# Long rows' lists in another order, in a kernel of four graph layers

## The chip, the cores and the metric

The kernel runs on one core of one Trainium2 chip. The core has five engines that run their own instruction streams in order and meet at semaphores: TensorE (PE, with the weight loads as PEld), VectorE (DVE), ScalarE (ACT), GpSimd (POOL) and SyncE (SP). SP issues nearly all of the plain transfers of this kernel, POOL the indirect ones. The metric is the device time of one execution in microseconds (us).

## The reference

There are 16 graphs of 1024 nodes with 64 features. Each graph has a sparse adjacency of 1024 x 1024; node i and node j are joined with a chance that falls with both numbers, so low nodes have long rows. Four layers follow each other, each with `h = relu(layernorm(x))` and a residual sum:

- layer 0: `m` from two dense steps of `h`, `msg = relu(adj @ m)`, then a gated unit (sigmoid and tanh) of `msg` and `h`;
- layer 1: `adj + 1` scaled on both sides by the root of the row sums, times `h @ kernel`;
- layer 2: of each node's neighbours some are removed by rank (where there are more than 10), and of the others' `h` a weighted sum of the quantiles 0.25, 0.5 and 0.75 is taken per feature, with interpolation; then two dense steps;
- layer 3: `(adj + 1) @ h` over its row sum.

Layer 2 is the one that matters here. Cut to its core:

```python
vals = jnp.where(valid[..., None], x[:, None, :, :], big)
sv = jnp.sort(vals, axis=2)
...
for tau, wt in zip(TAUS, QWEIGHTS):
    pos = jnp.clip(tau * (mf - 1.0), 0.0)
    ...
    q = gather(lo) * (1.0 - frac) + gather(hi) * frac
    agg = agg + wt * q
```

## The kernel before, in words

**Stages.** Each graph goes through thirteen stages, which are written as generators: fetch and load (read adj in strips of 128 rows, transpose it on PE, write adjT to DRAM), code, rank and cut (pack the neighbour flags into codes, rank the nodes by degree, remove neighbours), list (turn codes into lists of neighbour numbers), mid and next (layers 0 and 1; next ends with `tab`, the table of `h` rows in DRAM), gath (gather neighbours' rows from `tab`), sort and smalls (sort the gathered rows), sums (weighted sums into `agg`), rear (gather `agg` rows by rank into `zz`, layer 2's dense steps, layer 3). The graphs overlap: up to six have their tables in DRAM at once.

**Ranks and rows.** Nodes are ranked by degree. The first 128 ranks are the long rows, called heavy. Their lists have up to 143 entries and are gathered by 26 indirect transfers a graph into buffers `gh`; `gather_heavy` (L1584) issues them on POOL, PE transposes them and ACT copies them into `hb`, which DVE sorts. There are four `gh` buffers, each filled by two transfers. The other ranks, called light, are gathered by 49 transfers into `s` and two into `px`. At the end of a graph POOL gathers `zz` in eight transfers.

**The list stage, `lists` (L1135).** It reads `keys` (128 ranks x 128 codes for each of eight tiles of ranks). For the heavy tile the first 24 ranks (`HASHED`) are too long for 32 entries and are cut in segments, which `cuts` writes to DRAM as `seg` and reads back, spread over all partitions, as `sg2`. In the order of the program before:

1. `KH`: the 32 largest codes of each heavy row (four rounds of maximum and replacement, `rounds`); `KL`: the same for the light tiles.
2. The second round for ranks 24 to 127: `ch` decodes `KH` into 256 entries, four rounds find the 32 largest, `LH` holds them as numbers. The change calls these the far segments.
3. `sg2` is masked, `sc` holds its entries, and rounds find `LA` (32) and `LB` (16), the near lists of the segments of ranks 0 to 23.
4. ACT counts the entries of `LA`, `LB` and `LH` into `cs`; PE sums the counts over segments into `pl`; DVE makes `wa`, `wb_` from `LA`, `LB`, then `before` and `place` from `pl`; `m0` (in `mm`) is the row's length.
5. PE moves the segments' entries to their places, ACT copies them to `LC`.
6. `KL` is decoded into `cd`; flags; then the lists are written to the DRAM tensor `idx` in the order of `PARTS` (L53): 9 small transfers from `LC` and 7 from `LH`, in one loop on SP, after `LC`.
7. The light lists (`LF`, `L`, `idxL`), then `ih` reads `idx` back, PE transposes it, DVE copies it to `idxH`, which holds the gathers' row numbers. Then the weights `wl` and `w`.

A gather of a graph can start when its `idxH` and its `tab` are there and the light gathers of the graph before have been issued.

**What sets the order.** No order is written out by hand. `Order.run` (L278) keeps, for each stage, the next step: the engine that it is for and the tiles that it waits for. It takes the stage with the smallest value of `start` (when the planner's own clock says that the engine is free and the tiles ready) plus `lead`, and lets it emit instructions up to its next `yield`. So a negative lead puts a stage's steps earlier in the engine's stream. The table `LEAD` (L222) has an entry for a kind of stage: five leads for DVE, ACT, PE, POOL and SP in this order; a slope by graph number; four additions for the first four graphs; two for the last two. "stream0", "stream1" and "stream3" are the loads of adjT rows (`am`, three buffers) for layers 0, 1 and 3; "flag" and "keep" run once. What is emitted first for an engine runs first on it, whatever the chip's times are.

Of the kernel before, what the change touches and what calls it, by code (L numbers as in the profile page):

```python
# [9 lines left out]
F32 = mybir.dt.float32  # L10
F16 = mybir.dt.float16
# [4 lines left out]
AF = mybir.ActivationFunctionType  # L16
ALU = mybir.AluOpType
AX = mybir.AxisListType

P = 128  # L20
# [24 lines left out]
HASHED = 24  # L45
WIDE = 160
# [110 lines left out]
def in_two_buffers(lens, kept, moves, first=None):  # L157
# [62 lines left out]


LEAD = {  # L222
    "rear": ((-0.25, -0.25, 0.25, -11, -65.5), -0, (0, -0, -0, -0), (-0.75, -6.5)),
    "gath": ((-11, 0, 0, -4.5, 0.25), -0, (-1.5, -0, 0, 0), (0, -0.25)),
    "sums": ((0, 0, 4, 21.75, -163.5), 0, (-0.75, 0, -0.75, 0), (0, 21.25)),
    "next": ((0, 0, 0, 14, 1.25), -0, (-0.5, 0, -0, 0), (0, 0)),
    "mid": ((0, -0, 0, 1, 4), 0, (-1, 0, -0, 0), (-0, 0)),
    "code": ((-192, -107.5, -0.25, 10, 0), 0, (5, 0, 1, -2), (3, 0)),
    "rank": ((0, 0, -121.5, 9.5, 7.75), 0, (-3.25, 0, 0, -0), (0, 0)),
    "cut": ((0, -1.25, -95.25, 0, -83.75), 0, (0, 0, 0, 0), (0, -0)),  # L230
    "list": ((-0, -3.5, -1, -10, -33.5), 0, (1, 0, -0, 0), (0, 0)),
    "fetch": ((-68.25, -2.25, -21.25, -29.5, -149.75), 0, (-10.5, -31.25, 0, -1.75), (2, 16)),
    "load": ((-49.75, 0, -163, -2.75, 1.25), 0, (-7.75, -0.5, 0, 0), (1, 1)),
    "sort": ((0, -79.5, -0.5, 21.25, -30.5), -0, (0, 0, 0, 0), (0.25, -0.75)),
    "smalls": ((0, 12.25, 7.5, 1.25, 1.5), 0, (0, 0, 0, 0), (-1.75, 1)),
    "flag": ((4, -17, -4.25, -1.75, -4.5), 0.1, (0, 8.5, 0, -8), (0, 0.75)),
    "keep": ((23, -0.75, 32.5, 4.25, -26), -1.55, (-9.75, -22.25, 7.25, 3.5), (15, 3.75)),
# [3 lines left out]
}  # L241


# [227 lines left out]
def kernel(  # L471
# [127 lines left out]
    def lists_for_all():  # L599
        order = Order(B)  # L600
        V, A, T = Engine(nc.vector, "V", order), Engine(nc.scalar, "A", order), Engine(nc.tensor, "T", order)
        G_, S_ = Engine(nc.gpsimd, "P", order), Engine(nc.sync, "S", order)
# [5 lines left out]
        ap_, wp, qp = pool("ap", 1), pool("wp", 1), pool("qp", 1)  # L608
# [59 lines left out]
        for k in range(8):  # L668
            v = NBITS * 2.0**k
# [116 lines left out]
        net16, at16, _ = in_two_buffers((16,), (16,), NET16)  # L786
# [348 lines left out]
        def lists(b, S):  # L1135
            d = D[b % DEPTH]
            info, keys, sg2, raw = S["info"], S["keys"], S["sg2"], I32
            def decoded(dst, codes, n):

                y = dst.rearrange("p (n k) -> p n k", k=8)  # L1140
                k = codes[:, :, None].to_broadcast([P, n, 8])
                p8, c8 = (c[:, None, :].to_broadcast([P, n, 8]) for c in (dpow, dcol))
                V.tensor_tensor(y.bitcast(raw), k.bitcast(raw), p8.bitcast(raw), ALU.bitwise_and)
                yield ("V",)
                V.tensor_sub(y, y, c8)
                yield ("V",)

            fl = ap_.tile([P, 10 + NT], F32, name="fl", bufs=2)

            KH = ap_.tile([P, 32], F32, name="KH", bufs=1)  # L1150
            mk = ap_.tile([P, P], F32, name="mk", bufs=1)
# [3 lines left out]
            for t in range(1, NT):  # L1155
                yield ("V",)
                mk = ap_.tile([P, P], F32, name="mk", bufs=1)
                yield from rounds(ROUNDS[t], KL[:, COFF[t] : COFF[t] + CODES[t]], keys[:, t, :], mk)
            ch = ap_.tile([P, 256], F32, name="ch", tag="cd", bufs=1)
            yield from decoded(ch, KH, 32)  # L1160
            KH = ap_.tile([P, 32], F32, name="KH", bufs=1)
            mh = ap_.tile([P, 256], F32, name="mh", tag="mk", bufs=1)
            yield from rounds(4, KH, ch, mh)
            LH = ap_.tile([P, 32], F16, name="LH", bufs=2)
            V.tensor_scalar(LH, KH, 0.0, None, ALU.max)
            yield ("V",)

            yield "V", sg2
            V.tensor_tensor(
                sg2.bitcast(raw), sg2.bitcast(raw),  # L1170
# [7 lines left out]
            LA = ap_.tile([P, 32], F16, name="LA", bufs=2)  # L1178
# [4 lines left out]
            yield from rounds(2, LB, sc[:, 1, :], mra)  # L1183

            cs = ap_.tile([P, 3], F32, name="cs", bufs=2)
            for i, v in enumerate((LA, LB, LH)):
                ja = ap_.tile([P, 32], F16, name="ja", bufs=1)
                A.activation(ja[:, 0 : v.shape[1]], v, AF.Sign, accum_out=cs[:, i : i + 1])
            c16 = ap_.tile([P, 2], F16, name="c16", bufs=2)
# [10 lines left out]
            for w, v, k in ((wa, LA, SEG_A), (wb_, LB, SEG_C)):  # L1200
                V.tensor_tensor(
                    w, v[:, 0:k, None].to_broadcast([P, k, 16]),
                    bsel[:, 0, None, 0:16].to_broadcast([P, k, 16]), ALU.mult,
                )
                yield ("V",)
            yield "V", pl
            before = ap_.tile([P, 2], F32, name="before", bufs=2)
            V.tensor_scalar(before, pl[:, 2:4], float(SEG_A + 1), None, ALU.add)
# [28 lines left out]
            V.reduce_max(fl[:, 8:9], fe, AX.X)  # L1237
            yield ("V",)
            V.tensor_copy(fl[:, 9:10], LB[:, SEG_C : SEG_C + 1])
            yield "S", LC  # L1240
            base = 0
            for a0, n, e0, k, _, _ in PARTS:
                o = d["idx"][:, base : base + n * k].rearrange("h (a k) -> a h k", k=k)
                for src, col, lo, hi in ((LC, 0, 0, 16), (LC, WIDE, 16, HASHED), (LH, 0, HASHED, P)):
                    r0, r1 = max(lo, 2 * a0), min(hi, 2 * a0 + 2 * n)
                    if r0 < r1:
                        q = 0 if lo == HASHED else lo
                        S_.dma_start(
                            o[r0 // 2 - a0 : r1 // 2 - a0], src[r0 - q : r1 - q, col + e0 : col + e0 + k]
                        )  # L1250
                base += n * k
            for t in range(1, NT):
                o = OFFS[t] + 1
                ml = ap_.tile([P, P], F32, name="ml", tag="mk", bufs=1)
# [1287 lines left out]
```

## Time and profile before

| what | us |
|---|---|
| median of 5 runs | 2279.26 (2274.99 to 2291.03) |
| profiled execution | 2277.36 |
| its span, first to last instruction | 2275.2 |
| DVE busy | 1906.9 |
| POOL busy | 1523.2 |
| first heavy gather (`gh`) of graph 0 starts | 157.5 |
| last light gather (`s`) of graph 15 ends | 2212.9 |
| list of graph 0: first `KH` maximum to `idxH` | 100.1 to 148.5 |
| list of graph 2: the same | 323.4 to 410.7 |

All instructions that the planner emits carry one line number in the profile, that of a helper (L465), so the profile is read by tiles: `gh<-tab,idxH` is a heavy gather, `idx<-LC` a transfer of segments' lists. A wait is put down to the instruction or transfer that came last. The time of a POOL gather is that of writing its descriptors, not of the data's arrival.

### The profile page before, as it was taken

The page shows a single profiled execution, that of the slowest core. Times are in us where ns is not written, and L with a number is a line of the kernel's source. Part 1 is how long each engine was busy: PE and PEld are TensorE (multiplying, and loading weights), DVE is VectorE, ACT ScalarE, POOL GpSimd, SP SyncE. Part 2 cuts the span into 40 slices and gives each one's busy share as a digit, 9 for nine tenths or more (in the row PEclk, how much of TensorE's full clock was granted, in tenths as well). Part 3 has the DMA queues.
Part 4 walks back from the last instruction along what each step waited for, and adds up shares of the span by engine and source line. Part 5 has one row for each costly group of instructions (what it writes and reads, how often), then busy time and mean ns, then how long its engine had stood idle before and what let it go on. Part 6 is the DMA issues. An engine that isn't in the chain of part 4 may idle for free. (4 is left out here: it accounts for less than half of the span.)

```text
span 2275.2 us, 35564 instructions
## 1 busy us (share of the span) xinstructions
PE 1520.7 (67%) x9522; PEld 789.6 (35%) x9522; DVE 1906.9 (84%) x6317; ACT 1538.4 (68%) x5241; POOL 1523.2 (67%) x1428
## 2 busy tenths in 40 slices
PE   4876757676667767687776867666777575763324
PEld 3433324333343433334333433233343233331202
DVE  3546898898988988978998898899889899989882
ACT  6776786787777676768686677777766677554231
POOL 5017767466776776757676777777777677777771
PEclk6887777787777868677877778787877676785565
DMA  7766657677757766776766776876766666463441
GB/s 206 219 210 194 188 149 218 190 189 234 210 155 228 205 165 203 211 230 182 236 192 191 196 219 174 240 208 174 221 166 203 179 185 162 125 171 79 103 148 25
DMA packets 402724, 419.80 MB, mean 185 GB/s; under 512 B 176236, under 2 KB 313330, under 8 KB 402514
## 3 DMA queue, kind: packets, MB, share of 16 engines
q1 hardware_dynamic: 357426, 372.68, 53.6%
q0 software_dynamic: 45088, 44.75, 10.6%
q8 instruction: 78, 1.28, 0.2%
q14 instruction: 132, 1.08, 0.2%
HBM read 332.94 MB, written 84.34 MB: 183 GB/s over the span
## 5 line engine op out<-in xcount | busy, mean ns | idle before, releaser
L465 POOL DMA_INDIRECT s<-tab,idxL x784 | 867.0, 1106 | 239.0 <-issue 228.3
L465 POOL DMA_INDIRECT gh<-tab,idxH x416 | 449.7, 1081 | 340.3 <-DMA tab<-h 119.2
L465 DVE TENSOR_TENSOR hb<-hb 128x128 f32<-128x128 f32 (+10 forms) x1040 | 522.7, 538 | 17.4 <-ACT hb L465 12.8
L465 PE MATMUL bank<-ident,a 128*128 128x128 f32 x1024 | 197.0, 332 | 105.2 <-DMA a<-in_adj_dram 55.6
L465 POOL DMA_INDIRECT zz<-agg,posi x128 | 140.7, 1100 | 120.1 <-issue 35.1
L465 PE MATMUL bank<-am,tr 128*64 128x512 f32 x512 | 173.9, 793 | 65.8 <-DMA am<-adjT 33.9
L465 PE MATMUL bank<-am,hr 128*64 128x512 f32 x480 | 161.7, 780 | 79.8 <-ACT hr L465 44.1
L465 PE MATMUL bank<-am,m2x 128*64 128x512 f32 x512 | 165.0, 728 | 53.2 <-DMA am<-adjT 46.8
L465 PEld LDWEIGHTS bank<-ident,a 128*128 128x128 f32 x1024 | 142.3, 170 | 158.2 <-issue 55.3
L465 ACT COPY strip<-bank 128x512 f32<-128x512 f32 x256 | 146.7, 592 | 62.0 <-PE bank L465 47.4
L465 DVE TENSOR_TENSOR hb<-hb,hb 128x488 f32<-128x488 f32 (+7 forms) x368 | 173.4, 483 | 4.5
L465 ACT ACTIVATE s<-s,wl 128x64 f32<-128x64 f32 x624 | 166.7, 349 | 8.5 <-DVE s L465 8.5
L465 ACT ACTIVATE junk<-bank,nkey 128x1024 bf16<-128x1024 f32 x128 | 142.2, 1111 | 23.6 <-PE bank L465 21.4
L465 ACT ACTIVATE sgn<-strip,flat 128x1024 bf16<-128x1024 f32 x128 | 147.5, 1152 | 4.2 <-PE bank L465 1.2
L465 PE MATMUL bank<-cx,oh 128*128 128x133 f16 (+1 forms) x1280 | 144.1, 263 | 8.1 <-DVE oh L465 7.2
L465 PE MATMUL bank<-ident,gh 128*128 128x128 f32 x208 | 66.9, 346 | 122.0 <-DMA gh<-tab,idxH 115.1
L465 PEld LDWEIGHTS <-oh 128*128 128x128 f16 x1280 | 97.7, 110 | 46.6 <-issue 16.2
L465 DVE TENSOR_TENSOR o<-s 128x64 f32<-128x64 f32 (+6 forms) x208 | 95.2, 490 | 13.7 <-ACT s L465 7.4
L465 PE MATMUL bank<-wg,cat 128*128 128x256 f32 x256 | 99.0, 523 | 0.0
L465 PEld LDWEIGHTS bank<-ident,gh 128*128 128x128 f32 x208 | 31.2, 160 | 181.9 <-issue 134.1
L465 DVE TENSOR_TENSOR s<-o 128x192 f32<-128x192 f32 (+5 forms) x224 | 93.9, 447 | 0.0
L465 PE MATMUL bank<-am,ones 128*32 128x256 f32 x1024 | 92.1, 435 | 0.0
(443 smaller groups left out, 3737.9 us busy)
## 6 DMA issues: line engine op xcount, KB each, us to landing
am<-adjT SPq DMA_DIRECT2D x376, 512.0 KB
a<-in_adj_dram SPq DMA_DIRECT2D x128, 512.0 KB
adjT<-strip SPq DMA_DIRECT2D x128, 512.0 KB
s<-tab,idxL POOLq DMA_INDIRECT x784
gh<-tab,idxH POOLq DMA_INDIRECT x416
wb<-wd SPq DMA_DIRECT2D x32, 152.0 KB
X<-in_x_dram SPq DMA_DIRECT2D x16, 256.0 KB
x<-X SPq DMA_DIRECT2D x16, 256.0 KB
```

Source lines behind the costliest of these rows:

```text
L465: return f(*args, **kw)
```

## The change

Two things change. In `lists`, the second round of the far segments (step 2 above, from `ch` to `LH`) moves behind `wa` and `wb_`, just ahead of the wait for `pl`; ACT's count of `LH` moves with it. The transfers to `idx` are issued in two loops, all 7 from `LH` as soon as it is there and then the 9 from `LC` when that is there. And all 18 entries of `LEAD` have other numbers, so the order of all engines' streams is planned anew. The operations and their number stay.

```diff
 LEAD = {
-    "rear": ((-0.25, -0.25, 0.25, -11, -65.5), -0, (0, -0, -0, -0), (-0.75, -6.5)),
-    "gath": ((-11, 0, 0, -4.5, 0.25), -0, (-1.5, -0, 0, 0), (0, -0.25)),
-    "sums": ((0, 0, 4, 21.75, -163.5), 0, (-0.75, 0, -0.75, 0), (0, 21.25)),
...
-    "list": ((-0, -3.5, -1, -10, -33.5), 0, (1, 0, -0, 0), (0, 0)),
-    "fetch": ((-68.25, -2.25, -21.25, -29.5, -149.75), 0, (-10.5, -31.25, 0, -1.75), (2, 16)),
...
-    "stream0": ((6, 0, 0, 2.5, -14.75), -0.15, (-9.25, 16.75, 0, 7.5), (-2.25, 2)),
-    "stream1": ((8.75, -6, 11.25, 13.25, -2), 0.1, (3.5, 2.25, 0.75, -13.75), (-4.5, -5.75)),
-    "stream3": ((-2.75, -4.75, -23, 1.75, -52.5), 1.5, (0.5, 0.5, 0, -6.25), (-27, -8.5)),
+    "rear": ((-0.25, -0, 0.25, -12, 0), 0, (0, 0, 0, 0), (-2, -7.25)),
+    "gath": ((-26, -0.25, -0.25, -4.5, -0.75), 0, (-1.5, 0, 0, 0), (0, 0)),
+    "sums": ((0, 0, -9.75, 4.75, -175.5), -0, (-0.5, 0, -0, 0), (0.25, 37)),
...
+    "list": ((0, -3.5, -1, 0, -143.5), 0, (1, 0, 0, 0), (0, 0)),
+    "fetch": ((-65.5, 6, -1.5, -14.25, -207.75), 1.6, (0.5, 2, 8, -1), (2, 6.5)),
...
+    "stream0": ((6.5, -12.25, 11.25, 5.5, -44.5), 0.4, (8, -4.75, 33.75, 0), (-2.75, 0)),
+    "stream1": ((-10.25, -0, 11.5, -0, -2.25), -0.25, (-5.75, 3, 1.25, 2.75), (1.5, -1.5)),
+    "stream3": ((22.5, 5, 3.25, 4.5, -142.25), 2.5, (0, -1.75, -4, -6.5), (6.5, 0)),
 }
...
                 yield from rounds(ROUNDS[t], KL[:, COFF[t] : COFF[t] + CODES[t]], keys[:, t, :], mk)
-            ch = ap_.tile([P, 256], F32, name="ch", tag="cd", bufs=1)
-            yield from decoded(ch, KH, 32)
-            KH = ap_.tile([P, 32], F32, name="KH", bufs=1)
-            mh = ap_.tile([P, 256], F32, name="mh", tag="mk", bufs=1)
-            yield from rounds(4, KH, ch, mh)
-            LH = ap_.tile([P, 32], F16, name="LH", bufs=2)
-            V.tensor_scalar(LH, KH, 0.0, None, ALU.max)
-            yield ("V",)
-
             yield "V", sg2
...
-            for i, v in enumerate((LA, LB, LH)):
+            for i, v in enumerate((LA, LB)):
                 ja = ap_.tile([P, 32], F16, name="ja", bufs=1)
                 A.activation(ja[:, 0 : v.shape[1]], v, AF.Sign, accum_out=cs[:, i : i + 1])
...
+            ch = ap_.tile([P, 256], F32, name="ch", tag="cd", bufs=1)
+            yield from decoded(ch, KH, 32)
+            KH = ap_.tile([P, 32], F32, name="KH", bufs=1)
+            mh = ap_.tile([P, 256], F32, name="mh", tag="mk", bufs=1)
+            yield from rounds(4, KH, ch, mh)
+            LH = ap_.tile([P, 32], F16, name="LH", bufs=2)
+            V.tensor_scalar(LH, KH, 0.0, None, ALU.max)
+            yield ("V",)
+            ja = ap_.tile([P, 32], F16, name="ja", bufs=1)
+            A.activation(ja, LH, AF.Sign, accum_out=cs[:, 2:3])
             yield "V", pl
...
-            yield "S", LC
-            base = 0
-            for a0, n, e0, k, _, _ in PARTS:
-                o = d["idx"][:, base : base + n * k].rearrange("h (a k) -> a h k", k=k)
-                for src, col, lo, hi in ((LC, 0, 0, 16), (LC, WIDE, 16, HASHED), (LH, 0, HASHED, P)):
-                    r0, r1 = max(lo, 2 * a0), min(hi, 2 * a0 + 2 * n)
-                    if r0 < r1:
-                        q = 0 if lo == HASHED else lo
-                        S_.dma_start(
-                            o[r0 // 2 - a0 : r1 // 2 - a0], src[r0 - q : r1 - q, col + e0 : col + e0 + k]
-                        )
-                base += n * k
+            for src, ways in ((LH, ((0, 0, HASHED, P),)), (LC, ((0, 0, 0, 16), (WIDE, 16, 16, HASHED)))):
+                yield "S", src
+                base = 0
+                for a0, n, e0, k, _, _ in PARTS:
+                    o = d["idx"][:, base : base + n * k].rearrange("h (a k) -> a h k", k=k)
+                    for col, q, lo, hi in ways:
+                        r0, r1 = max(lo, 2 * a0), min(hi, 2 * a0 + 2 * n)
+                        if r0 < r1:
+                            S_.dma_start(
+                                o[r0 // 2 - a0 : r1 // 2 - a0], src[r0 - q : r1 - q, col + e0 : col + e0 + k]
+                            )
+                    base += n * k
```

More of the change, by code (lines that the diff above doesn't have):

```diff
@@ L222 @@
 LEAD = {
-    "rear": ((-0.25, -0.25, 0.25, -11, -65.5), -0, (0, -0, -0, -0), (-0.75, -6.5)),
-    "gath": ((-11, 0, 0, -4.5, 0.25), -0, (-1.5, -0, 0, 0), (0, -0.25)),
-    "sums": ((0, 0, 4, 21.75, -163.5), 0, (-0.75, 0, -0.75, 0), (0, 21.25)),
[L226 to L230, printed above, removed]
-    "list": ((-0, -3.5, -1, -10, -33.5), 0, (1, 0, -0, 0), (0, 0)),
-    "fetch": ((-68.25, -2.25, -21.25, -29.5, -149.75), 0, (-10.5, -31.25, 0, -1.75), (2, 16)),
[L233 to L237, printed above, removed]
[3 rows of a table removed]
+    "rear": ((-0.25, -0, 0.25, -12, 0), 0, (0, 0, 0, 0), (-2, -7.25)),
+    "gath": ((-26, -0.25, -0.25, -4.5, -0.75), 0, (-1.5, 0, 0, 0), (0, 0)),
+    "sums": ((0, 0, -9.75, 4.75, -175.5), -0, (-0.5, 0, -0, 0), (0.25, 37)),
+    "next": ((0, 0, 0, 9, 1.25), 0, (-0.5, 0, 0, 0), (-0.25, 0)),
+    "mid": ((0, 0, 0, -19.75, 3.25), 0, (-1, 0, 0, 0), (0, 0)),
+    "code": ((-383.75, -129.5, -0.25, -8.25, -5.75), 0, (4.5, 0, 1, -87.75), (0.5, -13.5)),
+    "rank": ((-0.5, 0, -146.25, 0.75, 6.75), 0, (-4.25, -1.5, 0, -0), (0, 0)),
+    "cut": ((0, -1.25, -79, -7.5, -88.25), 0, (0.25, 0.5, 0, 0), (0, -0)),
+    "list": ((0, -3.5, -1, 0, -143.5), 0, (1, 0, 0, 0), (0, 0)),
+    "fetch": ((-65.5, 6, -1.5, -14.25, -207.75), 1.6, (0.5, 2, 8, -1), (2, 6.5)),
+    "load": ((-12, 0, -167.5, -9, 1.25), 0, (-3.5, -0.5, 0, 0), (0, 1.5)),
+    "sort": ((0, -75.5, -58.75, 7.5, -50.25), 0, (0, 0, -0, 0), (0.75, -1.5)),
+    "smalls": ((0, 17, -1.75, 1.5, 0), 0, (0, 0, 0, 0), (-2, -28.5)),
+    "flag": ((-56.5, -1.75, 23.75, -4, 0), 2, (-1.75, -0.75, 4.75, -2.5), (11.5, -3.25)),
+    "keep": ((19.5, 29.25, 5.25, 26, 2.75), -0.15, (40.5, -3.25, -9, 3.5), (-0.5, -6.25)),
[3 rows of a table added]
 }
```

## The prediction

> **What bounds the kernel now.** I read the busy shares first, then the stretch between the first and the last gather, then POOL's own waits, and last the timelines of the two places where POOL waits for what a list hands over. Part 1 of the page and the windows view (PE, PEld, DVE, ACT, POOL, PE clock, DMA share, GB/s):
>
> ```profile
> PE 1520.7 (67%) x9522; PEld 789.6 (35%) x9522; DVE 1906.9 (84%) x6317; ACT 1538.4 (68%) x5241; POOL 1523.2 (67%) x1428
> 157.00:2213.00 2056.00, 1389.33 (x8620) 714.60 (x8619) 1818.09 (x5836) 1414.47 (x4898) 1485.81 (x1352) 0.76 0.66 188
> ```
>
> Shares alone name DVE. But POOL's 1352 gathers between 157 and 2213 us each have a gap of 0.30 us ahead of them that is put down to issue: 1485.8 + 1352 x 0.30 = 1891 us, 92% of the 2056, against DVE's 1818 (88%). From graph 3 on, the first heavy gather of a graph (tile gh) starts 0.3 to 2.6 us after the last light gather (tile s) of the graph before: 545.5 to 545.8, 671.2 to 671.5, and so on to 2094.7 to 2095.0. So POOL is the chain: 157.5 us until it can begin, 2055 us of gathers in order, and 62 us after the last light gather. Inside the 2056 us it waits 2056 - 1891 = 165 us. POOL's waits (us in total, times, longest):
>
> ```profile
> POOL s L465 <- issue: 228.3, 749, 0.3
> POOL gh L465 <- DMA tab<-h: 119.2, 1, 119.2
> POOL gh L465 <- PE bank L465: 99.3, 58, 10.9
> POOL zz L465 <- DVE hb L465: 28.9, 5, 9.9
> POOL zz L465 <- DMA agg<-s: 20.2, 2, 18.1
> POOL gh L465 <- DVE idxH L465: 9.8, 2, 9.3
> ```
>
> The second line is the start-up. The third is the ring of four gh buffers that PE's transposes empty. The last is the only line that names a list's result: one wait of 9.3 us, at graph 2, for idxH. Graph 2 in the timelines of SP, PE and POOL:
>
> ```profile
> 388.54 1.39 SPq L465 DMA_DIRECT2D idx<-LC  x2
> 390.04 0.65 SPq L465 DMA_DIRECT2D idx<-LH  x1
> ...
> 398.55 0.62 SPq L465 DMA_DIRECT2D idx<-LC  x1
> 399.28 0.39 SPq L465 DMA_DIRECT2D a<-in_adj_dram  x1
> 399.76 0.39 SPq L465 DMA_DIRECT2D adjT<-strip  x1
> 400.20 2.79 SPq L465 DMA_DIRECT2D am<-adjT  x3
> 403.09 0.41 SPq L465 DMA_DIRECT2D ih<-idx  x1
> 410.25 0.20 PE L465 MATMUL bank<-identh,ih 26*128 26x26 f16 x1 [11.23 <-DMA ih<-idx]
> 410.94 1.35 POOL L465 DMA_INDIRECT gh<-tab,idxH  x1 [9.30 <-DVE idxH L465]
> ```
>
> To see: sixteen small transfers take SP from 388.5 to 399.2, near and far ones mixed; three loads of 512 KB go ahead of ih; ih arrives 7.1 us after its issue; PE stands 11.2 us for it and POOL 9.3.
>
> **The change part by part.** The sums are made against the profiled execution: span 2275.2 us, time 2277.4, which is 1.9 us (0.1%) under the median of 2279.26. No instruction is added or removed on any engine: 16 transfers, three counting activations and the same DVE operations per graph.
>
> *Second round of the far segments, moved behind wa and wb_.* From the rows of groups:
>
> ```profile
> L465 DVE MAX8 KH<-mh 128x8 f32<-128x256 f32 x48 | 20.6, 428 | 1.7
> L465 DVE MATCH_REPLACE8 mh<-KH,mh 128x256 f32<-128x256 f32 x32 | 13.1, 408 | 0.0
> L465 DVE TENSOR_TENSOR ch<-KH,dpow 128x256 int32<-128x256 int32 x16 | 6.6, 415 | 0.0
> ```
>
> It is 0.415 + 0.42 (decode), 0.42 + 3 x 0.428 (maxima), 3 x 0.408 (replacements), 3 x 0.085 (their value loads), 0.18 (LH): 4.2 us of DVE a graph, 67 us in all, unchanged in sum. It moves past the and of sg2 and the near rounds, but it still stands ahead of before, place and so of LC. What it can win is the wait for pl. In graph 0 that wait is 4.39 us, in graph 2 none: DVE goes from wb_ at 372.8 to before at 373.5 on other stages' work. So in graph 2, the only list that POOL waits for, it wins 0; bounds 0 and 4.2. What it uncovers is the wait for sg2: the second of its loads is issued 3.3 us before the KL maxima end in graph 0, 5.1 in graph 15, 8.6 to 21.5 in the others, and seg, a transfer of the same kind, landed 2.7 us after its issue in graph 0. I take 0; if the landing takes ih's 7.1 us, it costs graph 0 3.8 us and graph 15 2.0, off POOL's chain. The mark that lets the next graph overwrite keys comes one block earlier; nothing on POOL waits for keys, so 0. ACT's count of LH (0.23 + 0.19 us) now stands just ahead of mm, which reads it: before and place (0.6 us) cover it, and if ACT is in a 1.1 us activation, DVE waits that long; DVE has room, so 0.
>
> *Far lists' transfers first.* Seven LH and nine LC issues take SP 10.5 us in graph 0 (126.19 to 136.68) and 10.6 in graph 2, 0.66 each. Seven of them, 4.6 us, now go before LC exists. They are hidden if SP has 4.6 us between LH and LC: in graph 2 LH would end near 373 and LC ends at 388.5, and SP issues two things in the last 3 us of that. Gain on idxH of graph 2: 4.6, bounds 0 (LH right in front of LC) and 4.6. In graph 0 the same 4.6 us fall on a wait too, by another road: DVE stands 8.97 us at idxH (until 148.34), and behind it in order stands the reciprocal of ln_vn, whose input ACT had ready at 143.2; from there go h, tab at 152.24 and the first gather at 157.46. That would start POOL up to 5.8 us earlier, but graph 2 waits for its own list, so these microseconds only lengthen that wait: I count 0, at most 5.8 if graph 2's wait goes entirely.
>
> *The table of leads.* All 18 entries change. POOL's own, gath and rear, hardly: -4.5 stays, -11 becomes -12. The largest on the path is list on S, -33.5 to -143.5: it puts LH's, LC's and ih's issue ahead of the loads of stream1 (-2.25) and stream0 (-44.5), behind only fetch (-207.75) and level with stream3 (-142.25). In graph 2 ih could then be issued when the last idx has landed, 399.2 + 2.1 (seg's 2.7 less its 0.6 of issue) = 401.3, and land by 404.0 if it takes seg's 2.7 us, instead of 410.2. Gain 6.2, of which I take 6.1; bounds 0 (if a load stays ahead, as am does now) and 6.2. idxH of graph 2 then comes 4.6 + 6.1 = 10.7 us earlier, at 400.0. The light gathers of graph 1 end at 401.6 now, at 395.8 if the start gives its 5.8, so POOL goes on at 400.2 and not at 410.9: **-10.7 us**. In the other graphs idxH is done 6 to 45 us before POOL wants it: 0. PE's other waits for ih (28.6 us in 9 in all, 11.2 of them in graph 2) leave 17.4 us that shrink by most of their length, but they come 20 to 40 us ahead of the heavy gathers, when POOL works on light lists; of that I take 1.5 us for the ring, bounds 0 and 17.
>
> Two leads have a price. Rear's 1 us more on POOL puts zz's eight gathers up to 1 us earlier in the queue, where they already wait for agg (67 us in the 12 gaps over 0.5 us before the last): 0 to 15 us, I take 0 because the last light transfer (agg<-s) and not the gathers' place sets when they run. The early list transfers hold what is behind them on SP; that is the slower rival.
>
> Sum: -10.7 - 1.5 = -12.2; **2279.3 - 12.2 = 2267 us** (-0.54%).
>
> The row against a rule: POOL with its 0.30 us gaps is 92% taken. The Trainium skill, Perfetto Trace Analysis, section Identifying the Most-Contended Engine, says for Vector, Scalar and GpSimd to take the engine with the highest occupancy as the bottleneck and to work on it first. By it DVE (84%) is the bound, POOL (67%) is not, and since the change leaves DVE's 1907 us as they are, the sum would be 0 and the time 2279. The back-to-back starts of gathers speak for the row.
>
> **The rivals.**
>
> *Absorbed: 2279.* POOL gets ahead at graph 2 and loses it again to the ring and to zz (99 + 67 us of waits, spread over all graphs), because DVE at 88% sets when agg and the sorted buffers are ready. For it: 1818 us of DVE work in 2056, only 15 us a graph free. Against it: in 14 of 16 graphs POOL's first heavy gather follows the last light one within 2.6 us. Price: all of 12.2 back, 2279; 2270 if a quarter is lost.
>
> *SP blocked: slower.* The place is SP's queue between LH's issue and ih's. SP already waits for LC 28.0 us in 9 graphs and for the landing of idx 5.5 us. With list at -143.5 it stands at LC and at the landing in every graph, and am, of which only three fit, is late for PE; PE's transposes of gh are behind the matmuls that wait. Each graph: up to 3.1 (28.0/9) + 2.1 us. If 2 us of these 5.2 reach POOL in 16 graphs, it is +32 - 12 = 2299; all of it, 2350. It decides from 0.8 us a graph (12.2/16). For it: PE waits for am 115 us in 86 waits already. Against it: SP spends 785 us waiting for PE to free am, so most loads have slack.
>
> *The new leads take steady waits too: 2240.* If the other 17 entries also save a sixth of the 165 us, 27 us, the time is 2240. For it: zz waits of 14.1, 9.9 and 9.6 us are single misplacements. Against: gath's T and P leads, which set the ring's order, stay at 0 and -4.5.
>
> **How the numbers follow.** The measured runs lie between 2274.99 and 2291.03, so about 0.5% (11 us) is what a measurement can tell from no change. Chances: forecast 0.36 (own range 2256 to 2277), absorbed 0.20, SP blocked or leads worse 0.26 (2291 to 2350), leads better 0.18 (2225 to 2255). Two thirds of the forecast's own range is faster than 2268: 0.24 + 0.18 = 0.42. Within 0.5%: the rest, 0.12, and 0.19 of absorbed, 0.31. Slower: 0.26 + 0.01 = 0.27. The range leaves out 1 in 10 at each side: 2236, inside the better leads, to 2304, inside the blocked queue.
>
> **What would show it.** Right: in SP's timeline seven LH issues in a row before nine LC; ih next to the last of them without am between; the 9.3 us wait of gh for idxH gone; the first gather before 157; DVE's idxH wait (26.1 us in 9) under 15. Wrong: gh for PE bank over 99 us, zz over 67, SP for ACT LC over 28, or a graph whose first heavy gather waits again for idxH or tab.

## The result, and the profile after

The changed kernel takes 2295.41 us (median of 29 runs, 2275.5 to 2306.45) beside 2281.66 us of the kernel before (55 runs): ratio 1.0057, 95% interval 1.0042 to 1.0072. It is 13 us slower, by a little more than the 0.5% that I had set as the bound; I had forecast 12 us faster. The profiled execution of after took 2306.75 us (span 2304.8), so it is 11 us above its kernel's median, while that of before (2277.36) is 4 us under the 2281.66; 29.6 us lie between the two spans, about 13 between the kernels. Here and below a difference in us is the ratio less one, times the median of before; it can be some us off the difference of the two medians. Three groups of the runs below (e1 to e4; g1 and h1 to h3; l1 and l2) met the chip at a lower clock, with the kernel before itself at 3084, 3148 and 3142 us, so their times can't be set beside 2280 us and are told as ratios alone.

Busy shares (part 1 of the page of after) and the stretch from its first heavy to its last light gather (windows view: bounds, length, PE, PEld, DVE, ACT, POOL, clock, DMA share, GB/s):

```profile
PE 1517.6 (66%) x9522; PEld 788.8 (34%) x9522; DVE 1907.5 (83%) x6317; ACT 1537.5 (67%) x5243; POOL 1553.2 (67%) x1428
174.60:2239.50 2064.90, 1373.57 (x8579) 708.09 (x8578) 1809.87 (x5798) 1405.83 (x4879) 1515.97 (x1352) 0.76 0.65 184
```

DVE's work is unchanged (1906.9 before). POOL begins at 174.6 instead of 157.5 us, and its same 1352 gathers take 1515.97 us instead of 1485.81. POOL's waits in after (us in total, times, longest; the first line is the start-up, which ends 0.3 us after graph 0's idxH is there):

```profile
POOL gh L465 <- DVE nz L465: 132.1, 1, 132.1
POOL gh L465 <- PE bank L465: 74.9, 56, 9.2
POOL zz L465 <- DMA agg<-s: 26.1, 2, 21.1
POOL s L465 <- DMA agg<-s: 14.0, 1, 14.0
POOL zz L465 <- DVE rs L465: 13.5, 1, 13.5
POOL zz L465 <- DVE nn L465: 12.8, 1, 12.8
POOL gh L465 <- DVE hb L465: 8.5, 3, 7.9
```

To see: the wait of 9.3 us for graph 2's idxH is gone, and the ring of gh buffers costs 74.9 for 99.3. The first of these is luck. idxH of graph 2 is there at 409.5 us, 1.2 us sooner than before and not 10.7, but POOL comes to it 12 us later: the last light gather of graph 1 ends at 413.4 us instead of 401.6. In DVE's and POOL's timelines of after:

```profile
409.28 0.19 DVE L465 CAST idxH<-bank 128x26 int32<-128x26 f16 x1
413.67 1.03 POOL L465 DMA_INDIRECT gh<-tab,idxH  x1 [0.30 <-issue]
```

Added up over all gaps of more than 0.5 us between the first and the last gather, POOL waits 145.5 us, 169.2 before. In sum the waits fell by more than I had said, by 23.7 us. The books of POOL close all the same at +29.6: first gather +17.1, waits -23.7, the gathers' own time +30.1, the short issue gaps +3.0, the tail +3.1. The gathers by groups, after and then before (count, busy us and mean ns):

```profile
L465 POOL DMA_INDIRECT s<-tab,idxL x784 | 887.4, 1132 | 252.6 <-issue 228.9 <-DMA agg<-s 14.0 <-DMA s<-tab,idxL 6.7
L465 POOL DMA_INDIRECT zz<-agg,posi x128 | 148.6, 1161 | 117.6 <-issue 33.5 <-DMA agg<-s 26.1 <-DVE rs L465 13.5
```

```profile
L465 POOL DMA_INDIRECT s<-tab,idxL x784 | 867.0, 1106 | 239.0 <-issue 228.3 <-DMA s<-tab,idxL 5.8 <-DVE hm L465 0.6
L465 POOL DMA_INDIRECT zz<-agg,posi x128 | 140.7, 1100 | 120.1 <-issue 35.1 <-DVE hb L465 28.9 <-DMA agg<-s 20.2
```

**The late start.** Graph 0 in the timeline of SP, after:

```profile
140.78 5.41 SPq L465 DMA_DIRECT2D idx<-LH  x7
146.29 4.66 SPq L465 DMA_DIRECT2D idx<-LC  x9
151.05 0.38 SPq L465 DMA_DIRECT2D a<-in_adj_dram  x1
151.49 1.36 SPq L465 DMA_DIRECT2D am<-adjT  x3
156.28 0.37 SPq L465 DMA_DIRECT2D tab<-h  x1
...
161.56 2.50 SPq L465 DMA_DIRECT2D am<-adjT  x2
164.11 0.42 SPq L465 DMA_DIRECT2D a<-in_adj_dram  x1
165.30 1.93 SPq L465 DMA_DIRECT2D am<-adjT  x2
167.29 0.40 SPq L465 DMA_DIRECT2D ih<-idx  x1
```

The seven LH transfers do stand first. But ih goes out 16.3 us after the last LC transfer (2.4 us after it in before), behind seven loads of am, and SP stands still ahead of two of their pairs (4.3 us before the first), all three am buffers being full. Over all graphs ih's issue stands 13.6 us behind the last idx issue, 7.2 before. The code says why: ih is emitted by the same generator only after the light lists' rounds and idxL, so a lead of -143.5 on S moves it no further ahead than DVE's and ACT's steps before it let it.

**Where the time is lost.** By the starts of the first heavy gathers the late start is made good by graph 3 (545.7 us after, 545.8 before), graph 6 begins level (949.7 and 948.1), and graph 10 begins 31.2 us late (1494.3 and 1463.1); from there to the last gather after is 4.6 us quicker. So the loss of this pair comes about in graphs 6 to 9. The windows of before and of after:

```profile
948.10:1463.10 515.00, 385.84 (x2346) 194.40 (x2342) 453.72 (x1478) 379.37 (x1298) 371.52 (x341) 0.78 0.72 205
```

```profile
949.70:1494.30 544.60, 371.66 (x2320) 187.07 (x2318) 465.08 (x1519) 381.01 (x1329) 384.60 (x341) 0.78 0.67 192
```

POOL's gathers there are 13.1 us longer and its waits 16.8 us longer (59.4 for 42.6). One of those waits, in the timelines of SP and POOL in after, at the start of graph 8:

```profile
1219.21 1.39 POOL L465 DMA_INDIRECT s<-tab,idxL  x1 [0.31 <-issue]
1223.30 0.38 SPq L465 DMA_DIRECT2D tab<-h  x1
1228.45 0.94 POOL L465 DMA_INDIRECT gh<-tab,idxH  x1 [7.86 <-DVE hb L465]
```

The table h of graph 8 goes out at 1223.3 us, in before at 1157.8; that of graph 9 at 1352.8, in before at 1246.6. Idx lists are not what POOL waits for: graph 8's idxH was there at 1195.0. The releaser named, DVE's hb, is inferred; from the issue of tab to the gather it is 5.2 us (5.4 in g3 and g4), as in graph 0 of before (5.2), where the profile names tab. A late table is not by itself a loss: graph 9's gathers start only 16.8 us after its table went out, 0.3 us behind the last light gather, and the tables of graphs 12 and 13, 77 and 76 us later than in before, hold nothing up either.

The two other large waits of the stretch are the zz waits of 13.5 and 12.8 us in the list above, of graphs 5 and 7. These three places mark the new order in every trace with it (g2 to g5, k1 and k2 are told below):

| POOL waits, us | after | g3, g4 | before | g2, g5, k1, k2 |
|---|---|---|---|---|
| zz of graph 5 | 13.5 | 16.2, 11.0 | 9.9 | 1.1 to 9.1 |
| first gh of graph 8 | 7.9 | 11.0, 10.9 | 0.3 | 0.3 |
| zz of graph 7 | 12.8 | 9.9, 9.8 | 3.7 | 2.8 to 5.4 |

In the pair they are 20.3 us of the 29.6 by which the stretch is longer. What makes the gathers in it 13.1 us longer isn't known.

### The profile page after: what moved, and what is told of

The parts are those of the page before. It is cut to its first block, busy times and chain, and to the rows that moved or that the text cites. A ratio compares the mean times of both kernels' runs of the same rounds, so it can differ in the third digit from the quotient of the medians.

```text
span 2304.8 us, 35556 instructions
## 1 busy us (share of the span) xinstructions
PE 1517.6 (66%) x9522; PEld 788.8 (34%) x9522; DVE 1907.5 (83%) x6317; ACT 1537.5 (67%) x5243; POOL 1553.2 (67%) x1428
## 5 line engine op out<-in xcount | busy, mean ns | idle before, releaser
L465 POOL DMA_INDIRECT s<-tab,idxL x784 | 887.4, 1132 | 252.6 <-issue 228.9
L465 DVE TENSOR_TENSOR hb<-hb 128x128 f32<-128x128 f32 (+10 forms) x1040 | 522.8, 538 | 21.5 <-ACT hb L465 16.9
L465 PE MATMUL bank<-ident,a 128*128 128x128 f32 x1024 | 204.7, 342 | 60.5 <-ACT strip L465 24.9
L465 POOL DMA_INDIRECT zz<-agg,posi x128 | 148.6, 1161 | 117.6 <-issue 33.5
L465 PE MATMUL bank<-am,tr 128*64 128x512 f32 x512 | 166.5, 763 | 62.3 <-DMA am<-adjT 33.4
L465 PEld LDWEIGHTS bank<-ident,a 128*128 128x128 f32 x1024 | 147.2, 175 | 121.5 <-ACT strip L465 42.3
L465 ACT COPY hb<-bank 128x128 f32<-128x128 f32 (+13 forms) x240 | 43.8, 282 | 97.5 <-PE bank L465 97.3
L465 PE MATMUL bank<-wg,cat 128*128 128x256 f32 x256 | 91.7, 491 | 0.0
```

What stands on the lines that cost most here:

```text
L465: return f(*args, **kw)
```

## The experiments

### Each part alone, the order planned anew

Four kernels, two of them run again as f1 and f2. The planner makes a new order for each.

```diff
 e1, f1: the changed lists(), with the old table LEAD
 e2, f2: the old lists(), with the new table LEAD
 e3:     old table; only the transfers in two loops, LH first
 e4:     old table; only the block ch ... LH moved behind wa and wb_
```

> The list stage as in the changed kernel, the table of leads as in the kernel before; the order is planned anew. If the moved block and the split transfers cost the 13 us (theory A), about 2294. If the new table costs them (theory B), 2277 to 2285, and the first heavy gather of graph 0 starts by 160 instead of 174.6. If every new plan scatters by chance (theory C), anything from 2265 to 2310, and the four runs of this set do not add up.

> The list stage as before, the new table of leads. Theory A: 2281. Theory B: 2290 to 2300, with the first heavy gather of graph 0 near 174. Theory C: anywhere in 2265 to 2310.

> Only the transfers split, seven LH ahead of nine LC, everything else as before. By the prediction's step the idxH of graph 2 comes 4.6 us earlier and POOL's wait there falls from 9.3 to about 5: 2277. Theory A: slower, 2285 or more. Theory B: 2275 to 2283. Theory C: no relation.

> Only the second round of the far segments moved behind wa and wb_; transfers and leads as before. The prediction's step says 0: 2281. Theory A puts 5 to 13 us here, because the block now stands between the near lists and LC: 2286 to 2294. Theory B: 2275 to 2285. Theory C: no relation.

> The list stage as in the changed kernel, the table of leads as in the kernel before, once more, since in the first set the kernel before itself took 3084 us (PE's stream stood still for up to 32 us at a time with nothing to wait for) and can't be set beside 2281. Theory A (the moved block and the split transfers cost the time): 2294. Theory B (the new table costs it, at the start and in graphs 4 to 9): 2277 to 2285, first heavy gather of graph 0 by 160. Theory C (every new plan scatters): anything from 2265 to 2310.

> The list stage as before, the new table of leads, once more. Theory A: 2281. Theory B: 2290 to 2300, first heavy gather of graph 0 near 174. Theory C: anywhere in 2265 to 2310, and the two runs' differences from the kernel before do not add up to the changed kernel's 13 us.

Measured: f1 2334.49 us beside 2276.58, ratio 1.0250 (1.0220 to 1.0279), 57 us slower; f2 2376.62, ratio 1.0427 (1.0395 to 1.0460), 97 us slower. In the group at 3084 us: e1 1.0156 (1.0112 to 1.0200), e2 1.0521 (1.0458 to 1.0584), e3 1.0118 (1.0056 to 1.0180), e4 1.0648 (1.0590 to 1.0706). So neither part gains by itself, and parts of 57 and 97 make a whole of 13: the effects don't add, and the change can't be read as a sum of a code part and a table part. The big waits sit elsewhere in each trace. In f2, one wait of 38.9 us for an index list in the last graph (its idxH is there at 2167.3 us; the releaser named is inferred):

```profile
2127.76 0.91 POOL L465 DMA_INDIRECT s<-tab,idxL  x1 [0.30 <-issue]
2167.61 0.95 POOL L465 DMA_INDIRECT gh<-tab,idxH  x1 [38.93 <-DVE nz L465]
```

In f1, it is one of 37.0 us of zz, which DVE's o released, and a table that came 26.1 us late for one graph. The first heavy gather starts at 159.1 us in f1 and at 175.2 in f2: the late start belongs to the new table.

### The order frozen

To take re-planning out, the order in which stages were picked was recorded (14,068 picks before, 14,084 after) and replayed pick for pick, so that no stage is re-ordered against another and only the named steps move:

```diff
-                    t = self.start(s[2], s[3]) + self.lead(s[0], s[2])
-                    if best is None or t < best[0] - 1e-6:
-                        best = (t, s)
-            s = best[1]
+            s = recorded(self)
```

g2 is before's order with the changed `lists`, except that there the seven LH transfers, too, wait for LC, since before's order has one step for all sixteen; g3 is after's order with the old `lists`; in g4 (after's order) and g5 (before's) the one step of ih stands right behind the transfers:

```diff
+            ih = ap_.tile([2 * NCOL, P], F16, name="ih", bufs=2)
+            yield "S", d["idx"]
+            S_.dma_start(ih, d["idx"].rearrange("h (c p) -> (h c) p", p=P))
             for t in range(1, NT):
                 o = OFFS[t] + 1
...
-            ih = ap_.tile([2 * NCOL, P], F16, name="ih", bufs=2)
-            yield "S", d["idx"]
-            S_.dma_start(ih, d["idx"].rearrange("h (c p) -> (h c) p", p=P))
```

> The planner is taken out: the order in which stages are emitted is that of the kernel before, pick for pick (14,068 picks replayed), and only the list stage's own steps stand in the new order (LA, LB, counts and places first, then ch to LH; the seven LH transfers ahead of the nine LC ones). No stage is re-ordered against another. Theory 1, the list code is neutral or slightly good by itself and all the loss comes from the new plan: 2272 to 2283 (down to -9.3 if the wait of POOL for idxH of graph 2 goes with the earlier transfers). Theory 2, the new order inside the list is what costs (LC and the places now stand ahead of the far rounds, the LH transfers hold SP): 2290 or more, and the waits of POOL for idxH grow.

> The mirror image: the emission order of the changed kernel, pick for pick (14,084 picks), with the list stage's steps and transfers in their old order (one empty step stands for the one that the change added). Theory 1 (the plan costs, the code does not): still 2290 to 2305, with the first heavy gather near 170 to 176 us, since the load of ih stays behind the loads of am in the plan. Theory 2 (the code costs): back to 2275 to 2285.

> The changed kernel with its emission order replayed; the one step that loads ih stands directly behind the idx transfers, ahead of the light codes' rounds and idxL, so that no load of am or a comes between them on SP's queue. The load went out 13.6 us after the last idx transfer on average over the graphs (7.2 before). Theory 3, the loss is the late ih: the first gather comes near 159 instead of 174.6, POOL's other waits for idxH shrink, and the time falls to 2278 to 2285. Theory 4, the late start is made good by graph 3 anyway (gathers of graph 3 start at 545.7 and 545.8 us in both traces) and the loss comes later, where POOL waits for the table h and for sorts: 2290 to 2298, unchanged within 0.3%. Against both: SP stands still until the idx rows have landed, some 2 to 4 us per graph, which the am loads behind it feel: up to +10.

> The same step moved in the kernel before, its emission order replayed. My prediction's step for the lead on S, done alone and in a plan that cannot move: the 9.3 us wait of POOL for idxH of graph 2 goes. If POOL's back-to-back gathers are the chain as I said: 2270 to 2275 (up to -10). If other waits take its place within a graph or two: 2279 to 2285. If the stop of SP at ih costs more than it gives: 2285 to 2295.

Measured beside 2274.62 us: g2 2295.78, ratio 1.0093 (1.0061 to 1.0124); g3 2318.03, 1.0197 (1.0162 to 1.0233); g4 2295.07, 1.0093 (1.0061 to 1.0125); g5 2277.25, 1.0010 (0.9985 to 1.0034).

*g2: the new order of the list costs 21 us in the old plan,* against theory 1. In its trace the last gather ends 16.9 us later than in before, and 16.1 of them are lost in graphs 3 to 5 (543.3 to 961.7 us, 545.8 to 948.1 before). It names a wait that is not there in before. ACT's waits in g2:

```profile
ACT ja L465 <- DVE LH L465: 40.8, 11, 9.8
```

The groups of before have 0.5 us of idle time for the same instruction:

```profile
L465 ACT ACTIVATE ja<-LH 128x32 f16<-128x32 f16 x16 | 3.7, 229 | 0.5
```

The count of LH has no `yield` of its own. Moved with LH, it enters ACT's stream where DVE's step for LH is emitted, and ACT, which runs in order, stands there for up to 9.8 us until DVE has caught up. In after the same wait is 2.1 us in 4, so the new order all but removes it. I had put this count at 0. Whether these 40.8 us of ACT make the 21 us was not tested.

*g3: the old list in the new plan stands 45 us above before,* 13 us over the upper end of theory 1, and theory 2, which g2's time alone would have fitted, falls. Beside the new list in the same plan (2295.07 in g4, same group; 2295.41 in after) it is 23 us slower. So the same change of the list costs 21 us in the old order and gains some 23 in the new one: order and list are fitted to each other, which f1 and f2 say too. The stretch of graphs 6 to 9 is long in every trace with after's order (544.6, 537.9 in g4, 541.5 in g3) and short in every trace with before's (515.0, 519.4 in g2, 513.8 in g5; 517.3 and 520.2 in k1 and k2 below): it goes with the order, whichever list stands in it. In g3 and g4 the tables of graphs 8 and 9 are as late as in after (1227.1 and 1355.0; 1222.2 and 1351.0).

*g4: the late ih is not the loss.* Issued 1.9 us behind the last idx transfer, it brings idxH of graph 0 only from 174.3 to 168.3 us, because PE reaches its transpose only at 166.6 us and DVE its copy at 168.1; the first gather follows at 168.6, and graph 3 starts at 545.3. The time is that of after as far as two groups can be compared (ratios 1.0093 and 1.0057, intervals that overlap). Theory 4 holds.

*g5: no gain from the wait that I had priced.* In graph 2 ih is issued 2 us behind the last idx transfer, and idxH comes 87.4 us after the keys instead of 92.3. The wait shrinks:

```profile
400.42 0.95 POOL L465 DMA_INDIRECT gh<-tab,idxH  x1 [5.62 <-DVE idxH L465]
```

9.30 us became 5.62, and the time shows no gain (-3.4 to +7.7 us by the interval). The 3.7 us are small for this test: the interval excludes that all of them reach the end, but not that half of them do.

### Is POOL the chain? More of its work, and more of DVE's

Before's order replayed, with two more light gathers a graph into tiles that nothing reads (h3, k1), or with 24 more DVE instructions a graph among the light gathers, of two inputs (h1, k2) or of one (h2):

```diff
+            nc.gpsimd.indirect_dma_start(
+                out=spare[g], out_offset=None, in_=D[b % DEPTH]["tab"][:, :],
+                in_offset=bass.IndirectOffsetOnAxis(ap=S["idxL"][:, 0:1], axis=0),
+            )
...
                     gather(b, keys[0:m, j, at], S["idxL"][0:m, OFFS[t] + j : OFFS[t] + j + 1])
+                    if not (nth := S["nth"] + 1) % 4:
+                        nc.vector.tensor_tensor(scr, scr, scr, ALU.max)
+                        nc.vector.tensor_tensor(scr, scr, scr, ALU.max)
```

In h2 the added lines are `nc.vector.max(out=top8, in_=scr)`.

> The kernel before, its emission order replayed, with two more light gathers per graph (one ahead of each network's) into tiles that nothing reads: 32 times (1.11 us and the 0.30 us to the next issue) = 45 us of POOL. My prediction's main statement, POOL's back-to-back gathers are the chain from 157 us to the tail: +38 to +45 (ratio 1.017 to 1.020). If POOL's waits (169 us) take the half of it or more, because what it waits for (a sort's bank, the table h, an index list) is itself the chain there: +5 to +25.

> The kernel before, its emission order replayed, with 24 more DVE instructions per graph (two behind every fourth light gather's issue): a tensor by tensor maximum over 128x128 f32, 287 ns each by the rows of before, 110 us in all, on a tile of its own that nothing else reads. In the profile of before a gather with no two-input DVE instruction beside it takes 949 ns, one with 900 ns or more of them 1199 ns; 211 us of all gathers' time lie above 943 ns, over 1204 us of overlap, 0.175 us per us. Theory 6, two-input work of DVE stretches the gathers: POOL's busy time between first and last gather rises from 1486 to 1500 to 1515, and the time is 12 to 25 us above that of the run with one-input instructions. Rival, only DVE's time counts: both runs within 5 us of each other, gathers unchanged.

> The same places and the same number, but the eight largest of 128x128 f32 (one input, 295 ns each, 113 us in all). DVE is busy 84% of the span before, so 113 us have room in 365 us of idle time, but not where its sorts run without a gap. Theory 6: gathers as before (busy 1478 to 1494), time 2280 to 2330. Rival, every DVE instruction beside a gather stretches it: busy 1500 or more here too.

> The same kernel as h3, again, since the chip of that call ran the kernel before at 3148 us with 1121 us of POOL's waits, where POOL bounds nothing. On a chip that runs the kernel before near 2277 us: 32 more light gathers are 45 us of POOL (32 times 1.11 + 0.30). POOL the rigid chain, as I predicted: ratio 1.017 to 1.020. If half or more of it disappears in POOL's 169 us of waits: 1.002 to 1.011.

> The same kernel as h1, again, for the same reason (on that chip the three altered kernels stood at 1.012 to 1.013 alike). On a chip that runs the kernel before near 2277 us: theory 6, the 384 two-input DVE instructions (110 us) lengthen the gathers: POOL's busy time between first and last gather 1500 to 1515 (1479 to 1494 in three profiles of this plan), ratio 1.012 to 1.035. Rival, only DVE's time counts: busy stays under 1495, and the one-input instructions would cost the same.

In the group at 3148 us h1 (1.0029 to 1.0211), h2 (1.0035 to 1.0229) and h3 (1.0043 to 1.0207) can't be told apart. Beside 2271.85 us: k1 2289.28, ratio 1.0061 (1.0031 to 1.0091); k2 2312.87, ratio 1.0161 (1.0124 to 1.0198). The added gathers, and the stretch of gathers, in k1:

```profile
L1800 POOL DMA_INDIRECT spare<-tab,idxL x32 | 38.1, 1192 | 9.8 <-issue 9.8
155.40:2225.90 2070.50, 1397.64 (x8617) 722.11 (x8614) 1817.40 (x5836) 1414.62 (x4901) 1510.66 (x1384) 0.75 0.64 187
```

Of 48 us of POOL (38.1 + 9.8), 13.9 us reach the end, 0.29 of them (0.15 to 0.43 by the interval); its waits shrink from 169.2 to 147.7 us, and the other gathers from 1485.8 to 1472.5, the latter without a cause that I can name. POOL is not a rigid chain. The page of k2, and its stretch:

```profile
PE 1538.2 (66%) x9522; PEld 801.0 (35%) x9522; DVE 1997.8 (86%) x6702; ACT 1537.2 (66%) x5241; POOL 1524.7 (66%) x1428
158.00:2257.50 2099.50, 1407.40 (x8628) 725.94 (x8622) 1909.04 (x6220) 1410.26 (x4885) 1487.09 (x1352) 0.75 0.63 184
```

DVE is busy 90.9 us longer, the time 36.6 us: 0.40 (0.31 to 0.50 by the interval; 0.33 of the 110.7 us that the added instructions last). The intervals of the two shares overlap, so which engine's time counts more is not settled. The gathers are not longer (1487.09 for 1485.81), so theory 6, as I had sized it, falls; POOL waits 213.1 us instead of 169.2.

A third number of this kind needs no edit. The granted clock differs between executions of one and the same kernel. Over 47 runs of before (0.753 to 0.775) the time falls by 7.0 us per 0.01 of clock (standard error 1.8, r = -0.50), over 31 of after by 8.1. If all of the time went with PE's clock, it would be 2273 x 0.01 / 0.763 = 29.8 us; so about 0.23 of it does. That is a correlation, not an edit: the clock can also follow what the execution does. POOL 0.29, DVE 0.40, PE perhaps 0.23: this suggests, and does not show, that the end is set by a chain that runs through all three by turns.

### What the longer gathers come from

Laid over DVE's instructions, a gather of before with no two-input instruction beside it takes 949 ns, one with 900 ns or more of them 1199 ns; of the 1493 us of all 1360 gathers 211 lie above 943 ns each, 241 in after. The Trainium skill, SBUF — State Buffer, section SBUF: two separate sides, says that DVE instructions with two SBUF inputs and GpSimd instructions that read SBUF take one shared pair of ports as an exclusive lock for a whole instruction. The rows above agree in direction. From it I concluded that the length of a single DVE instruction counts and that k2's short ones (287 ns) cost nearly nothing. So the sorts' two-input instructions of 600 columns and more were cut in two, the order replayed; and after was profiled again:

```diff
-            return f(*args, **kw)
+            for part in halved(args) if name == "tensor_tensor" and self.letter == "V" else (args,):
+                got = f(*part, **kw)
+            return got
```

> The changed kernel once more, for a second profile. In the first pair of profiles the 29.6 us between the spans fall apart as: first gather 17.1 us later; POOL's waits of over 0.5 us between first and last gather 23.7 us shorter (145.5 for 169.2); the gathers themselves 30.1 us longer in sum (s 1132 ns for 1106, zz 1176 for 1110, gh 1089 for 1081); short gaps +3, tail +3.1. Theory 5: the longer gathers belong to the plan and not to one execution: busy time of POOL between first and last gather 1505 to 1520 again (1485.9 before), zz 1165 to 1185 ns, waits 140 to 160, first gather 168 to 176. Rival, noise of one execution: busy 1480 to 1500, zz 1090 to 1130 ns.

> The kernel before, its emission order replayed, with each two-input DVE instruction of the sorts that has 600 columns or more (384 of them, 780 to 1204 ns) cut into two of half the columns; the same work in 384 more instructions. By the profile of before, a gather's time goes with the longest two-input DVE instruction beside it: 949 ns without one, 957 with one under 300 ns, 1006 up to 500, 1082 up to 700, 1211 up to 900, 1270 to 1285 above. Theory 7, the length of one instruction counts and not the sum (which is why 384 instructions of 287 ns lengthened nothing): some 430 gathers fall from about 1250 to about 1060 ns, POOL's busy time between first and last gather from 1486 to 1390 to 1430. For the time: POOL's 80 us by the 0.31 of the run with more gathers (13.9 us for 45) is -25; the cuts cost DVE up to 384 x 154 ns (704 columns take 886 ns, 384 take 554) = 59 us by 0.33 (36.6 us for 110) is +20: 2255 to 2285 beside 2277. Rival, the longer gathers have another cause: busy stays 1475 to 1495 and the time is 10 to 20 us longer.

> The same cut in the changed kernel, its emission order replayed. POOL's gathers were 30 us longer in its profile than in that of before (1516.0 for 1485.9; 1502.9 and 1520.3 in two other profiles of the same order). Theory 7: its busy time falls more than that of before does (to 1405 to 1440), and of the 13 us between the two kernels at most 6 stay between their two cut versions. Rival, the loss lies in the places of the waits: the two cut versions stand 10 to 18 us apart as the uncut ones do.

Measured, in the groups at 3148 and 3142 us: g1 1.0144 (1.0044 to 1.0245), l1 1.0015 (0.9977 to 1.0053), l2 1.0181 (1.0108 to 1.0255). There only 640 to 710 us of two-input work lie beside gathers (1204 in the profile of before), so the sums are smaller for all. The gathers between first and last take 1386.4 us in l1, beside 1389.8 in h2 and 1391.4 in h3 without its spare ones, which have the long instructions: the cut shortens next to nothing, against theory 7. In l2 they take 1370.5, beside 1395.7 in g1, 25 us less. The two cut versions stand as far apart (1.0015 and 1.0181) as the uncut ones there (1 and 1.0144). l1 and l2 disagree on the gathers, and what makes a gather long stays open; only that long gathers go together with two-input DVE work is seen. g1 could not show whether the longer gathers belong to the new plan. What speaks for it is that all three traces of 2304 to 2312 us with after's order have them (1516.0, 1502.9 in g3, 1520.2 in g4), and none of the four with before's order and the same 1352 gathers (1485.8, 1493.6, 1478.8, and 1487.1 in k2).

## Why the prediction was wrong

Two steps failed: that POOL is the chain, and that what feeds the list of graph 2, and all that the other leads move, stays where it was. In the pair of profiles the terms came out as waits -23.7 us (forecast -12.2), start +17.1 (taken as 0), and, none of them in the sum, the gathers' own time +30.1, the short gaps +3.0 and the tail +3.1.

*POOL is the chain, and a wait taken from it comes off the end.* This step failed, whatever the list does. Its reading of the trace was right, gather follows gather from graph 3 on, but a queue that is never empty is not yet a rigid one: 48 us more POOL work cost 13.9 (k1), and 3.7 us less of the very wait that I priced gained nothing measurable (g5). The rival "absorbed" had this mechanism (what one wait loses, others give back), but I gave it 0.20, and its time, 2279, was not the one measured either.

*idxH of graph 2 comes 10.7 us earlier, so POOL does too.* The list is shorter by nearly that: from the first piece of keys to idxH it takes 82.7 us in after (326.8 to 409.5) and 92.3 before (318.4 to 410.7), 9.6 less, with ih next behind the last transfer. But in the new order these keys come 8.4 us later, so idxH is there only 1.2 us sooner, and POOL begins graph 2 at 413.7 us, 2.8 later than before: the term of -10.7 was not there. I had taken what feeds the list as fixed while all 18 leads changed.

*Lead on S.* That list's lead of -143.5 brings ih's issue next to the landing of idx holds in graph 2, where I priced it, and in 8 and 15: ih goes out 1.6 to 2.2 us behind the last idx issue. In no other graph it does (5.3 to 26.4 us); in graph 0 ih waits behind seven am loads. A lead moves a step in a queue, not past the steps of its own generator.

*Start-up, counted 0 to -5.8.* It was +17.1, and the new table makes it (f2), but it is paid back by graph 3 and, by g4's 6 us, worth nothing that could be measured at the end.

*The second round moved, 0.* Not so in the old plan (g2, where the far transfers stand first as well: +21 us, with a new wait of 40.8 us of ACT at the count); in after this wait is 2.1 us. I priced ACT's 0.4 us and not what is queued behind it.

*The rival "SP blocked or leads worse".* It was the right side for the wrong place: SP waits for LC 5.2 us in after (28.0 before) and PE for ih 15.8 (28.6 before). The order is worse in graphs 6 to 9, at three places of POOL's queue that come back in every trace with it: the late table h of graph 8 (7.9 us in after, 0.3 before) and the zz of graphs 5 and 7 (13.5 and 12.8, 9.9 and 3.7 before). Which entries of the table put these waits there was not tried, so that cause stays open.

*The signs that I named.* LH in a row first: seen. The 9.3 us wait gone (by luck, as told above), DVE's idxH wait under 15 (10.8), gh for PE bank under 99, zz under 67 (60.9): all as hoped, with the time going the other way. The first gather before 157 (174.6) and a graph that waits again for idxH or tab (graphs 0 and 8): the two that spoke against me. *The rule that I weighed* (the Trainium skill, Perfetto Trace Analysis, Identifying the Most-Contended Engine: the highest occupancy first, so DVE) fits the shares measured, 0.40 for DVE and 0.29 for POOL, at least as well as my reading did, but their intervals overlap; neither engine is the bound alone.

*Readings that were off.* "behind only fetch" left out sums, whose lead on S (SP) is -175.5. gath's lead on T (PE) does not stay at 0 but becomes -0.25. In graph 1, too, idxH was only just in time (POOL waited 0.5 us), so "6 to 45 us before POOL wants it" does not hold for all the others. No run prices the first two. And spread evenly, the chances as stated put the ends of the range at 2242 and 2327, not at 2236 and 2304.

## What to carry to other kernels

Before a wait is priced at its length, ask how much of that engine's time reaches the end at all: some dummy work on it (48 us on POOL, 91 on DVE here) gives the share, with its interval, and the spread of the clock between runs gives a hint of PE's. Where a planner sets the order, a change of code and a change of its table can't be costed apart: replay the old code and the new in each of the two orders (here the same code costs 21 us in one and gains 23 in the other), and look for single instructions that ride in another engine's step, since they block the queue that they land in. Compare two kernels by stretches between like events, and only then by waits: here the sum of waits fell by 24 us, a wait that was to go went for another reason, and the loss of the pair came about in four graphs of sixteen.

## What the runs showed of the hardware

In three groups the kernel before took 3084 to 3148 us, at a clock of 0.67 to 0.69 instead of 0.75 to 0.78, and PE stood still with nothing to wait for that the profile shows. PE's waits in g1:

```profile
PE bank L465 <- issue: 378.3, 179, 27.5
```

In the trace of after this wait is 1.4 us in 1. It is not a trait of a chip, since two chips ran the kernel before near 2273 us in one group and above 3080 in another; its cause wasn't found.

In the profile of before 644 of the 1360 gathers last 930 to 950 ns, and the longest 4707: a spread that the means of 1081 to 1126 ns hide.
